# Two convolutional bottleneck layers on one core: stage borders with statistics summarized ahead, first images normalized on two engines, a plain first tile in the fused stage, and a divided last store

## Chip, cores and metric

The kernel runs on one core of a Trainium2 chip. The metric is device time in microseconds (us) of one execution. The engines are named as in the profile: PE (matmul), PEld (weight load, beside PE), DVE (vector), ACT (scalar), POOL (GpSimd), SP (sync); "ACTq" and "SPq" are the sequencers of ACT and SP while they issue transfers. The "granted clock" is the share of PE's full clock that the profile records; "half clock" is 0.50 of it.

## The reference

Two identical layers follow each other. Cut to what matters:

```python
# x: (64, 1024, 14, 14) fp32; P = 256
def layer(x, w1, b1, g1, be1, w2, b2, g2, be2, w3, b3, g3, be3, residual_scale):
    out = relu(bn(conv(x,   w1, b1, 1x1), g1, be1))    # 1024 -> 256
    out = relu(bn(conv(out, w2, b2, 3x3), g2, be2))    # 256 -> 256
    out = bn(conv(out, w3, b3, 1x1), g3, be3)          # 256 -> 1024
    return relu(x + softplus(residual_scale)[0] * out)
# bn: mean and variance over the whole batch and both image axes
```

A batch norm over the whole batch is a barrier: no value of the next convolution may be normalized before the last value of this one is known. These barriers are the "borders" of this document.

## The kernel before

Images are taken in pairs, as T = 32 tiles of PX = 392 pixels, and 256 channels lie in two slots of 128 partitions. Conv1 runs as sums of products with fewer multiplications (`Conv1`, seven products instead of eight), conv2 as a Winograd-like scheme over groups of 8 images (`combine`, `products`, `finish`). The statistics of conv3 are not taken from its output but from a Gram matrix of its input (`gram`, `conv3_stats`), so that in layer 0 conv3, the residual and conv1 of layer 1 run interleaved, in the "fused" stage. In layer 1 the last stage is conv3 and the residual alone. These are the parts that the change touches.

```python
# ---- border conv1 -> conv2, and conv2 -> gram: all 32 statistics, then ten tiny operations
def aggregate(stats, n):
    mv = small.tile(...)
    for o in range(n):
        nc.vector.bn_aggr(mv[:, o, :], stats[:, o, :, :].rearrange("p t f -> p (t f)"))
    return mv

def affine(mv, n, par, g, be, conv_bias=None):
    # ... tiles cut
    nc.vector.tensor_scalar(v, mv[:, :, 1], EPS, None, ALU.add)
    nc.scalar.activation(sd, v, AF.Sqrt)
    nc.vector.reciprocal(r, sd)
    # ... one Newton step, scale, shift: eight more operations on DVE, cut

# ---- start of conv2: both slots normalized on ACT, then combined
norm(0, aff)
ahead, acc = combine(*pairs[0]), None

# ---- end of each group in conv2 (finish, pair (0, 5)): statistics after the last row
nc.vector.tensor_add(out_rows[0], a, fa)
nc.vector.tensor_add(out_rows[3], d[:, :, :full], fb[:, :, :full])
for o in range(MS):
    y = y_grp[:, o, g].rearrange("p h l -> p (h l)")
    for c in range(GI // G):
        nc.vector.bn_stats(stats[:, o, g * (GI // G) + c, :], y[:, c * PX : (c + 1) * PX])

# ---- after conv2: loads for the next stages, then the scale and shift
w3 = load_w3(one, b)                  # issued by SP
if b == 0:
    w1 = load_w1(one, b + 1)          # four transfers, issued by ACT
aff = affine(aggregate(stats2, MS), MS, pb, G2, BE2)
# ...
crow = pool.tile([P, M], FP, tag="crow", name="crow")
nc.sync.dma_start(out=crow, in_=pars[b][:, NPAR:])     # subtracted in gram
# ...
made = [conv3(psum, 0, o, w3) for o in range(2)] if b == 1 else ()

# ---- fused stage: conv3 runs 28 + 14 steps alone before conv1 joins
a, c = stream(first_convs()), stream(last_convs())
step = 7 * CS // 2
for i in range(step + LAG):
    next(c)

# ---- a tile of the last stage ends with one store, issued by GpSimd
nc.gpsimd.dma_start(out=out[t], in_=xt.rearrange("p s f -> p (s f)"))
```

## Time and profile before

| | before |
|---|---|
| median of 4 runs (of the later comparison) | 2213.81 us |
| span of the profiled execution | 2210.7 us |
| first matmul | 6.67 us |
| conv1 of layer 0 ends on PE | 312.20 us |
| PE gap conv1 to conv2, layers 0 and 1 | 12.52 and 12.65 us |
| conv2 end to first transpose of gram, layers 0 and 1 | 11.00 and 10.91 us |
| last gram product to first conv1 matmul, layer 0 | 40.23 us |
| last relu to end of span | 9.89 us |

The table is read off the timeline of PE: a gap is the time from the end of one matmul to the start of the next. The prediction shows the timelines inside these gaps. The list of waits of PE: its columns are the waiting group, what ended the wait, the total in us, how often, and the longest:

```profile
PE ps L470 <- DVE sums L450: 25.2, 2, 12.7
PE ps L583 <- ACT y L396: 22.4, 4, 11.0
```

Line 470 is the first matmul of conv2 and line 583 a transpose of gram. Two waits of conv2, one for each layer, are 25.2 us, and the waits of the transposes 22.4 us. The list shows no slow clock and no thin stretch: the 40 us before the fused stage hardly appear here; what fills them has to be read from the table of stretches.

### The profile page before, as it was taken

The numbers are of one execution on the slowest core, as the hardware profiler recorded it, in microseconds if no ns is written. First come the engines' busy times: TensorE is split into PE (matmuls) and PEld (weight loads), VectorE is DVE, ScalarE is ACT, GpSimd is POOL, SyncE is SP. The second block draws the span as 40 slices with busy tenths as digits, with TensorE's granted clock in tenths as the row PEclk, the third lists the DMA queues.
The fourth block names the chain that finished last, engine by engine and source line by source line (L and its number), as shares of the span: only waits on it lengthen the run. The fifth ranks groups of instructions, "written<-read, shape, count | busy, mean of one in ns | idle before, by whom it ended". The sixth has DMA issues, their size and how long they took to land.

```text
span 2210.7 us, 27233 instructions
## 1 busy us (share of the span) xinstructions
PE 2125.5 (96%) x10648; PEld 1808.1 (82%) x10648; DVE 1431.1 (65%) x2591; ACT 724.5 (33%) x1391; POOL 250.9 (11%) x350
## 2 busy tenths in 40 slices
PE   8999979999998989999999999799999799999997
PEld 4555549999997879999999999699999797555554
DVE  5676557788775656676666666678878544444443
ACT  1111133111105045555555555611111221444443
POOL 0000000000001133333333333000000000000000
PEclk9999989999999989999999999899999899999999
DMA  7655424555534424444444442355555501778874
GB/s 288 254 200 201 173 94 178 186 198 183 187 141 161 153 100 167 172 175 172 165 164 172 176 175 117 148 191 191 191 190 191 197 13 57 294 302 310 314 295 175
DMA packets 44289, 409.44 MB, mean 185 GB/s; under 512 B 5504, under 2 KB 5760, under 8 KB 11392
## 3 DMA queue, kind: packets, MB, share of 16 engines
q1 hardware_dynamic: 29664, 287.06, 35.6%
q0 software_dynamic: 8448, 67.11, 7.4%
q10 hardware_dynamic: 6048, 53.52, 5.8%
q8 instruction: 84, 1.38, 0.3%
q14 instruction: 45, 0.37, 0.0%
HBM read 289.18 MB, written 118.49 MB: 184 GB/s over the span
## 4 chain that ended last, share of the span: by engine, by line
PE 72%; issue 20%; DVE 4%; DMA 2%; POOL 1%; ACT 1%; POOLq 0%; SPq 0%; ACTq 0%
PE ay L135 14%; PE cy L135 7%; PE ap L135 7%; PE ps L481 6%; PE ps L475 6%; PE ps L470 6%; PE ps L477 6%; PE ps L483 6%; PE cp L135 4%; PE ax L135 3%; PE cx L135 2%; PE bx L571 2%; PE ps L135 1%; DMA y<-in_w 1%; PE bp L572 1%
## 5 line engine op out<-in xcount | busy, mean ns | idle before, releaser
L135 PE MATMUL ps<-y,w 128*128 128x392 f32 x1024 | 339.1, 494 | 0.0
L135 PEld LDWEIGHTS ps<-y,w 128*128 128x128 f32 x1024 | 195.2, 191 | 142.8 <-issue 1.5
L645 DVE SCALAR_TENSOR_TENSOR x<-ps,scale,x 128x392 f32<-128x392 f32 x256 | 159.7, 625 | 174.2 <-PE ps L135 174.2
L234 ACT ACTIVATE cu<-cy,scale 128x196 f32<-128x196 f32 x384 | 158.7, 423 | 227.9 <-PE cy L135 225.4
L646 ACT ACTIVATE x<-x,shift 128x392 f32<-128x392 f32 x256 | 158.9, 622 | 177.4 <-DVE x L645 177.4
L135 PE MATMUL ay<-at,w1s 128*128 128x196 f32 (+1 forms) x752 | 209.7, 382 | 1.2 <-ACT au L234 1.0
L503 DVE TENSOR_TENSOR f<-ps,ms 128x448 f32<-128x448 f32 x192 | 113.3, 600 | 148.7 <-PE ps L483 80.7
L470 PE MATMUL ps<-sums,u 128*128 128x224 f32 (+1 forms) x768 | 172.1, 347 | 25.2 <-DVE sums L450 25.2
L475 PE MATMUL ps<-r,u 128*128 128x224 f32 (+1 forms) x768 | 173.6, 347 | 0.0
L481 PE MATMUL ps<-r,u 128*128 128x224 f32 (+1 forms) x768 | 173.3, 347 | 0.0
L494 ACT ACTIVATE ms<-ps 128x448 f32<-128x448 f32 (+1 forms) x80 | 42.0, 525 | 392.2 <-PE ps L470 392.2
L135 PEld LDWEIGHTS ay<-at,w1s 128*128 128x128 f32 x752 | 136.0, 190 | 36.6 <-ACT au L234 4.6
L470 PEld LDWEIGHTS ps<-sums,u 128*128 128x128 f32 x768 | 137.3, 190 | 26.3 <-ACT t L410 13.1
L234 ACT ACTIVATE x<-x,shift 128x392 f32<-128x392 f32 x256 | 145.5, 614 | 31.1 <-POOL x L367 29.3
L477 PE MATMUL ps<-r,u 128*128 128x192 f32 (+1 forms) x768 | 154.1, 322 | 0.0
L483 PE MATMUL ps<-r,u 128*128 128x192 f32 (+1 forms) x768 | 153.3, 321 | 0.0
L367 POOL TENSOR_TENSOR x<-x,cu 128x392 f32<-128x392 f32 x128 | 130.6, 1021 | 189.3 <-DVE x L341 187.0
L341 DVE SCALAR_TENSOR_TENSOR x<-cp,scale,x 128x196 f32<-128x196 f32 x256 | 106.8, 417 | 67.2 <-PE cp L135 67.2
L475 PEld LDWEIGHTS ps<-r,u 128*128 128x128 f32 x768 | 141.8, 190 | 1.3
L481 PEld LDWEIGHTS ps<-r,u 128*128 128x128 f32 x768 | 137.0, 189 | 1.5
L477 PEld LDWEIGHTS ps<-r,u 128*128 128x128 f32 x768 | 132.9, 189 | 1.1
L483 PEld LDWEIGHTS ps<-r,u 128*128 128x128 f32 x768 | 132.0, 188 | 1.1
(161 smaller groups left out, 3666.4 us busy)
## 6 DMA issues: line engine op xcount, KB each, us to landing
u<-u SPq DMA_DIRECT2D x96, 1280.0 KB, 5.5
x<-in_x SPq DMA_DIRECT2D x62, 1568.0 KB, 6.6
mid<-x ACTq DMA_DIRECT2D x32, 1568.0 KB, 5.1
x<-mid SPq DMA_DIRECT2D x32, 1568.0 KB, 6.6
out<-x POOLq DMA_DIRECT2D x32, 1568.0 KB, 6.2
u<-y POOLq DMA_DIRECT2D x24, 320.0 KB, 6.5
u<-spare POOLq DMA_DIRECT2D x24, 320.0 KB, 3.0
x<-in_x SPq DMA_DIRECT2D x4, 784.0 KB, 6.6
```

The costliest lines, as they stand in the source:

```text
L135: tc.keep_in_program_order(nc.tensor.matmul(*args, **kw))
L234: tc.keep_in_program_order(nc.scalar.activation(*args, **kw))
L341: nc.vector.scalar_tensor_tensor(v, bank, self.scale[:, o : o + 1], v, ALU.mult, ALU.add)
L367: nc.gpsimd.tensor_add(v, v, self.u12)
L470: nc.tensor.matmul(m[:, o, :n], w(s, D1D2), sums[:, s].rearrange("p l c -> p (l c)"), start=(s == 0), stop=(s == MS - 1),)
L475: nc.tensor.matmul(odd, w(s, D1), r[:, s, :, WH:], start=(s == 0), stop=False)
L477: nc.tensor.matmul(odd[:, :, : WH - 1], w(s, D3), r[:, s, :, WH + 1 :], start=False, stop=(s == MS - 1))
L481: nc.tensor.matmul(even, w(s, D2), r[:, s, :, :WH], start=(s == 0), stop=False)
L483: nc.tensor.matmul(even[:, :, 1:], w(s, D0), r[:, s, :, : WH - 1], start=False, stop=(s == MS - 1))
L503: nc.vector.tensor_tensor(f[:, o].rearrange("p r (i q c) -> p q (r i) c", i=GI, q=2)[:, :, :lines], eos[o][:, :, :n].rearrange("p q (l c) ...
L645: nc.vector.scalar_tensor_tensor(v, ps, scale[:, o : o + 1], v, ALU.mult, ALU.add)
L646: nc.scalar.activation(v, v, AF.Relu, bias=shift[:, o : o + 1])
```

## The change

The intent is to shorten the serial chain at each border. The kernel's author describes it so: borders between stages, with statistics summarized ahead, first images normalized on two engines, first fused tile plain; sums of conv1 not pinned. (The diff does not touch the sums of conv1, so that last point has nothing of its own to test.) Two more edits are in the diff: the very first tile is loaded in four parts, and the last store is divided in four and moved from GpSimd to SP. The core of the diff; the reworked PSUM pools and the reordering inside `combine` and `products` are cut.

```diff
-    def aggregate(stats, n):
+    def summarize(stats, half, end, count):       # early statistics -> one entry
+        ...
+    def aggregate(stats, first):
+        n = stats.shape[1]
         for o in range(n):
-            nc.vector.bn_aggr(mv[:, o, :], stats[:, o, :, :].rearrange("p t f -> p (t f)"))
+            nc.vector.bn_aggr(mv[:, o, :], stats[:, o, first:, :].rearrange("p t f -> p (t f)"))
@@ affine: sqrt reads mv directly, eps as bias; two multiplications joined
+        nc.scalar.activation(sd, mv[:, :, 1], AF.Sqrt, bias=eps)
         nc.vector.tensor_scalar(v, mv[:, :, 1], EPS, None, ALU.add)
-        nc.scalar.activation(sd, v, AF.Sqrt)
@@ start of conv2
-        norm(0, aff)
-        ahead, acc = combine(*pairs[0]), None
+        half = 8
+        norm(0, y_grp[:, 0, 0], aff)                              # ACT, slot 0
+        norm_vector(1, y_grp[:, 1, 0, :half], aff)                # DVE, half of slot 1
+        ahead = combine(*pairs[0], lambda: norm(1, y_grp[:, 1, 0, half:], aff))
+        acc = None
...
-            acc = finish(g, pair, products(now), acc)
+            acc = finish(g, pair, products(now, k == 0), acc)     # first: slot by slot
@@ end of a group in conv2: a statistic per row and slot, rows 1 and 2 already earlier
+                for item, f, more, k in zip(done, (fa, fb), acc, (0, 3)):
+                    n = RT if k == 0 else full
+                    for o in range(MS):
+                        column(item, f, o)
+                        nc.vector.tensor_add(out_rows[k][:, o], more[:, o, :n], f[:, o, :n])
+                        stat(o, k)
+                if g == NG - 2:
+                    summarize(stats, 4 * (NG // 2), 4 * (NG - 1), GPX // 4)
@@ gram: the first normalization in two pieces
+                if normed == 0:
+                    px.insert(1, CH * P)
@@ gram to fused: the first tile as in layer 1, without the seven-product scheme
-                    made = [conv3(psum, 0, o, w3) for o in range(2)] if b == 1 else ()
+                    made = [conv3(psum, 0, o, w3) for o in range(2)]
+                first = residual(psum, xpool, b, 0, w3, aff, made)
@@ fused
-            for t in range(T):
+            for t in range(1, T):
-        step = 7 * CS // 2
-        for i in range(step + LAG):
+        for i in range(LAG):
@@ residual, last tile
+        step = 2 if b == 1 and t == T - 1 else CS
...
+            if (o + 1) % step == 0:
+                queue = nc.gpsimd if step == CS else nc.sync
@@ start
-        pair = [load_x(xpool, 0, t, 2) for t in range(2)]
+        pair = [load_x(xpool, 0, t, 4 if t == 0 else 2) for t in range(2)]
```

## The prediction

> **What bounds the kernel now.** I read the engine table first, then the list of who waited for whom (PE alone), then a table of stretches cut at the gaps of PE, then the timeline inside each gap. The engine table says who leads:
>
> ```profile
> PE 2125.5 (96%) x10648; PEld 1808.1 (82%) x10648; DVE 1431.1 (65%) x2591; ACT 724.5 (33%) x1391; POOL 250.9 (11%) x350
> ```
>
> PE is busy for 2125.5 of 2210.7 us, so only 85 us of idle time can be won, plus what PE loses when it restarts slowly. Inside a stage nothing can be won: the table of stretches has PE at 69.00 of 69.00 us within conv2. The same table, cut at the borders (columns: stretch, its length, busy time of PE, PEld, DVE, ACT, POOL, granted clock, DMA share, GB/s):
>
> ```profile
> 312.20:324.70 12.50, 0.00 (x0) 0.01 (x1) 8.47 (x21) 10.24 (x11) 0.00 (x0) 0.68 0.80 315
> 324.70:331.00 6.30, 6.28 (x19) 5.85 (x20) 6.30 (x11) 6.30 (x8) 0.00 (x0) 0.54 0.00 1
> 660.40:671.40 11.00, 0.01 (x1) 0.03 (x1) 8.76 (x24) 2.04 (x3) 0.20 (x4) 0.71 0.73 273
> 780.10:806.50 26.40, 19.06 (x85) 15.48 (x86) 17.87 (x51) 12.88 (x30) 9.32 (x11) 0.85 0.32 123
> 1401.00:1413.65 12.65, 0.00 (x0) 0.03 (x1) 9.27 (x22) 8.95 (x10) 0.00 (x0) 0.68 0.78 311
> 1749.40:1760.20 10.80, 0.00 (x0) 0.00 (x0) 8.69 (x24) 1.94 (x3) 0.20 (x4) 0.71 0.78 308
> ```
>
> Four gaps of 11 to 12.7 us with no PE work, each followed by some 6 us at about half clock (0.54), and one thin stretch of 26 us. What fills a gap is the timeline (start, length, engine, line, operation). Conv1 to conv2, layer 0:
>
> ```profile
> 312.84 1.28 ACT L701 ACT_TABLE_LOAD   x1
> 313.45 1.02 DVE L689 BATCH_NORM_AGGREGATE mv<-stats 128x2 f32<-128x192 f32 x1
> 316.53 4.86 ACT L396 ACTIVATE y<-y,shift,scale 128x1568 f32<-128x1568 f32 x3 [1.61 <-DVE shift L717]
> 321.99 1.09 DVE L426 TENSOR_TENSOR r<-t 128x896 f32<-128x896 f32 x1
> 324.72 1.83 PE L470 MATMUL ps<-sums,u 128*128 128x224 f32 x4 [12.52 <-DVE sums L450]
> ```
>
> It is one serial chain: aggregate all 32 statistics, ten tiny operations 0.2 us apart, two normalizations of 1.69 us, combination, column sums, first matmul. Conv2 to gram, layer 0:
>
> ```profile
> 660.98 0.86 DVE L534 TENSOR_TENSOR y<-fb,f 128x672 f32<-128x672 f32 x1
> 661.88 3.84 DVE L538 BATCH_NORM_STATS2 stats<-y 128x6 f32<-128x392 f32 x8
> 665.63 1.89 DVE L689 BATCH_NORM_AGGREGATE mv<-stats 128x2 f32<-128x192 f32 x2
> 669.57 3.28 ACT L396 ACTIVATE y<-y,shift,scale 128x1568 f32<-128x1568 f32 x2 [1.61 <-DVE shift L717]
> 671.40 1.30 PE L583 MATMUL ps<-ident,y 128*128 128x128 f32 x5 [11.00 <-ACT y L396]
> ```
>
> Here 5.7 us are statistics.
>
> **The Trainium skill.** (1) "TensorE: Matmul & The Clock Gate", What's actually happening: after an idle window of about 3.4 us, free running, the clock is halved until a busy window. The trace agrees: 0.54 after the gap, 1.00 from 331 us. So shorter gaps of 5 to 7 us still pay the slow restart. (2) "VectorE: DVE Perf Modes", The perf-mode tier table: tensor_scalar on fp32 in SBUF runs at 2x, tensor_tensor at 1x. Trace: tensor_scalar 128x256 took 288 ns, tensor_tensor 128x448 617 ns. (3) "ScalarE: Activation LUTs", What ACT_TABLE_LOAD costs: 1283 ns; the trace has the same, at 312.84. (4) "DMA: Bandwidth & Descriptors", Anatomy of one DMA: about 2 us fixed per transfer, so a short last transfer cannot fall below that; the last store of before landed 5.4 us after its issue.
>
> **Part by part.**
>
> *Conv1 to conv2, layer 0.* Aggregating 3 entries (one a summary) in place of 32: 1.02 us to about 0.15 (estimate, in proportion to elements). But the square root must wait for the table load, to 314.12, so it starts at 314.13 and not 314.71; with it seven more steps of 0.2 us and not eight: shift ready at 315.75, not 316.53, 0.8 us won. Then: ACT normalizes slot 0 (1.69) while DVE does 896 elements of slot 1 in two tensor_scalars (0.62 each by the 288 ns row, estimate), hidden. DVE then combines slot 0 alone: two stt (0.50 + 0.43) and a half-size add (0.62). PE can start with the eight slot-0 products at 1.69 + 0.95 + 0.62 + 0.1 = 3.35 us after shift, where before it took 8.2. Slot 1 is ready some 1.6 us later, while these 16 instructions at half clock take 5.7 us, so PE is then fed. PE starts at 319.1, not 324.72: **5.6 us**.
>
> *The same border, layer 1.* No table load: the first aggregate (1400.77) no longer delays the last statistics, the second shrinks by 0.87, v is off the chain: shift at 1403.9 and not 1405.33. PE at 1407.2, not 1413.65: **6.4 us**.
>
> *Conv2 to gram.* The eight statistics after the last row become one per half row: behind the last product come a column (0.51), an add of 336 (0.45), one statistic (0.45), two aggregates of 5 entries (0.2 each). But the four statistics of rows 1 and 2 (1.9 us) now lie ahead, in a stretch where DVE has little room (654.1 end of the pair before): I get the last statistic at 661.9, shift at 664.0 and not 669.57: 5.5 us. The split of the first norm lets PE start 0.5 us after shift and not 1.8, but slot 1's rest still comes 3.75 us after; worth 0 to 1 us. Against it: the subtraction after the transposes needs crow, whose transfer is issued at 662.4 whatever DVE does:
>
> ```profile
> DMA to landing us min/median/max: 4.7/5.5/6.4
> ```
>
> (for crow, 6.4 in layer 0, 4.7 in layer 1). It lands near 668.5; first gram product at 669.5, not 674.67: **5.2 us**, and in layer 1 at about 1757.8, not 1763.57: **5.7 us**.
>
> *Gram to the fused stage.* Before, from the last gram product (766.2) to the first conv1 matmul (806.5) are 40.2 us: statistics 13.9, then 42 steps of conv3 alone, with 13.9 us of PE work (0.33 us a step) in 26.4: 2.9 us waiting for the scale, half clock, and waits of 0.9 to 2.2 us on the loop PE, ACT, DVE, POOL. After: layer 1 of before already shows what this becomes. There, two plain products stand ahead of the statistics, and gram end to the end of the tiny products took 1850.0 to 1863.15 = 13.1 us with them; the plain tile followed without a gap, 24 instructions of 0.33 us plus 1.9 for the slow clock = 9.8. Then only 14 steps of conv3 run alone; the steady rate alone was 3.13 us for 7 steps, with the conv1 sums in the way 7 to 8 us. Sum 13.1 + 9.8 + 7.5 = 30.4, against 40.2: **10 us**, 7 to 13. The plain tile costs 10.5 us of PE and not 9.2, which is in this sum. The lead of conv3 over conv1 stays 14 steps into tile 1, so the tail is as before.
>
> *Start.* The first tile in quarters: before, the first matmul waited for its weights (6.67 us) that shared the transfer engines with x rows of 6.3 KB; with rows of half that, perhaps 2 us earlier, at half clock, and part is lost again behind later tiles: **0.6 us**.
>
> *End.* The last tile leaves in four stores. The last is 392 KB and not 1568: 2.2 us of transfer and 0.2 of issue saved: **2.4 us**.
>
> *Hidden.* The summaries (four aggregates of some 0.5 us and small operations, 3 us of DVE per stage) run where DVE is 65 to 78% busy; statistics per row have the same elements. The sums of conv1 are not touched by the diff; unpinned, the scheduler may place them differently.
>
> Sum: 5.6 + 6.4 + 5.2 + 5.7 + 10 + 0.6 + 2.4 = 35.9 us. From 2214.1 that is 2178; I say **2179**, for small new stalls.
>
> **Rivals.** (a) A transfer replaces the chain. The conv2 filters land 5.8 us after issue at the earliest:
>
> ```profile
> DMA to landing us min/median/max: 5.8/8.0/10.6
> ```
>
> that is 318.1 and about 1406.9, only 1.0 and 0.3 us ahead of my PE starts. If these or crow land later, 3 to 6 us of the gain go: 2183. (b) DVE becomes the bound at the borders: the 2x mode fails for the half normalization, or DVE drags the extra statistics; 1 us per border: 2184. For it: DVE is 79% busy at the end of conv2. Against it: the largest costs removed are DVE's own. (c) The shorter gaps escape the half clock: five restarts at 2.5 us each would give up to 10 us more, about 2169. Against it: gaps of 4 to 7 us contain an idle window nearly always. (d) The fused lead-in stalls as before on its loop: loss of 5 us, 2184.
>
> **Range and chances.** The borders go by about 1 us each, together, and the fused lead-in by 3; with the clock's phase 3 more. So 2171 to 2189. Faster by over 2% needs under 2169.8, that is 44 us, over half of all idle time: 0.08. Slower needs a broken schedule: 0.01.
>
> **What would show it.** PE gaps: about 6.9 us at both conv1 borders and 4 to 5 at both conv2 borders; sqrt right after the table load in layer 0; the subtraction of gram waiting for crow; 28 to 32 us from last gram product to first conv1 matmul; conv2 still without PE waits; 2 us less after the last matmul; half clock still at each border. Wrong would be: conv2 or the fused stage longer by over 2 us, or restarts with no half clock.

## The result, and the profile after

| | before | after |
|---|---|---|
| median | 2213.81 us (2212.21 to 2214.30, 4 runs) | 2177.43 us (2175.48 to 2178.76, 4 runs) |
| ratio | | 0.9836, 95% interval 0.9819 to 0.9853 |
| span of the profiled execution | 2210.7 us | 2175.1 us |
| mean granted clock | 0.983 | 0.990 |

A ratio is the mean time of one kernel's runs over that of the other's of the same rounds, so it is not quite the ratio of the medians. The gain of 36.4 us, or 1.6%, lies within the 2% that count as the same.

The engine table of the changed kernel:

```profile
PE 2123.2 (98%) x10624; PEld 1802.2 (83%) x10624; DVE 1432.1 (66%) x2648; ACT 720.8 (33%) x1387; POOL 243.6 (11%) x342
```

PE's busy time fell by only 2.3 us (the prediction shows 2125.5), while the span fell by 35.6. So nearly all that was won is idle time of PE: 85.2 us before, 51.9 us after. The waits of PE in the changed kernel, with the columns as before:

```profile
PE ps L513 <- DVE r L454: 14.1, 2, 7.3
PE cp L622 <- DVE zt L642: 6.2, 5, 1.6
...
PE cy L640 <- ACT y L401: 6.0, 1, 6.0
PE ps L640 <- ACT y L401: 5.5, 3, 4.8
```

The first line stands where 25.2 us stood: conv2 now starts after the combined rows of slot 0 (line 454) and no longer after the column sums. The waits of the transposes (line 640) fell from 22.4 us to 12.0: 6.0 and 5.5 in the two rows shown, and 0.5 in a third. The gap in conv1 to conv2 of layer 0 and what follows it, as a table of stretches (stretch, length, busy time of PE, PEld, DVE, ACT, POOL, granted clock, DMA share, GB/s), with the stretch between gram and the fused stage below:

```profile
312.32:319.62 7.30, 0.00 (x0) 0.00 (x0) 5.41 (x17) 5.83 (x10) 0.00 (x0) 0.69 0.81 311
319.62:326.00 6.38, 6.38 (x20) 6.05 (x21) 6.28 (x10) 6.38 (x7) 0.00 (x0) 0.55 0.62 263
759.53:789.20 29.67, 27.99 (x122) 18.82 (x121) 18.54 (x52) 7.79 (x17) 2.63 (x3) 0.94 0.28 109
```

The same view of the kernel before, for the last of these stretches:

```profile
766.25:806.48 40.23, 32.34 (x146) 25.80 (x146) 23.04 (x65) 13.14 (x31) 9.30 (x11) 0.83 0.21 80
```

Between gram and the fused stage PE is busy for 4.35 us less and idles 6.2 us less (7.9 us before, 1.7 after): together the 10.6 us. Less busy time is not only less work: its clock there is also higher, 0.94 against 0.83. After the gap of conv1 to conv2, the clock is still about half (0.55) for 6 us.

Inside the first border (start, length, engine, line, operation; in square brackets, how long the engine had been idle and what ended that):

```profile
312.96 1.28 ACT L783 ACT_TABLE_LOAD   x1
...
313.58 0.24 DVE L772 BATCH_NORM_AGGREGATE mv<-stats 128x2 f32<-128x18 f32 x1
...
314.26 0.29 ACT L783 ACTIVATE sd<-mv,eps 128x2 f32<-128x2 f32 x1
...
315.96 0.75 DVE L405 TENSOR_SCALAR y<-y,scale,shift 128x896 f32<-128x896 f32 x1
...
318.95 0.62 DVE L454 TENSOR_TENSOR r<-t 128x448 f32<-128x448 f32 x1
319.62 1.75 PE L513 MATMUL ps<-r,u 128*128 128x224 f32 x4 [7.30 <-DVE r L454]
```

The aggregate reads 18 numbers and not 192 (three entries of six), and takes 0.24 us where 1.02 stood. The square root now starts 0.02 us after the table load has ended, so the load, and not the aggregate, sets the chain. DVE's half of slot 1 takes 0.75 us (and 0.63 for its second operation), hidden beside ACT. The one addition ahead of PE covers 448 elements, not 896.

The second border, conv2 to gram in layer 0, same columns:

```profile
656.76 2.08 ACTq L118 DMA_DIRECT2D w<-in_w  x4
...
657.18 0.29 DVE L772 BATCH_NORM_AGGREGATE mv<-stats 128x2 f32<-128x30 f32 x1
...
658.88 0.29 ACT L783 ACTIVATE sd<-mv,eps 128x2 f32<-128x2 f32 x1 [5.22 <-issue]
...
663.91 0.29 DVE L890 TENSOR_SCALAR crow<-crow 128x256 f32<-128x256 f32 x1 [3.36 <-DMA crow<-in_par]
...
665.15 1.20 PE L622 MATMUL cp<-zt 128*128 128x257 f32 x2 [1.57 <-DVE zt L642]
```

Two things stand here that the kernel before did not show as a loss. The aggregate is done at 657.47, but the square root runs only at 658.88, right after ACT's sequencer has issued four weight transfers (656.76 to 658.84). And DVE waits 3.36 us for the transfer of `crow`.

A third thing is in no wait: the clock after the restart. The table of stretches for the first 10 us from the first transpose on, in layer 0 and layer 1, columns as above, for the kernel before:

```profile
671.40:681.40 10.00, 9.78 (x55) 8.50 (x56) 6.40 (x13) 10.00 (x10) 1.08 (x2) 0.81 0.19 76
1760.10:1770.10 10.00, 9.61 (x42) 8.14 (x43) 2.72 (x4) 10.00 (x8) 0.00 (x0) 0.63 1.00 425
```

And for the changed kernel:

```profile
661.33:671.33 10.00, 7.95 (x31) 6.48 (x32) 3.73 (x7) 7.33 (x8) 0.54 (x1) 0.56 0.68 264
1729.89:1739.89 10.00, 9.26 (x47) 7.64 (x48) 3.40 (x6) 10.00 (x8) 0.00 (x0) 0.74 1.01 420
```

The granted clock (the third number from the end) fell from 0.81 to 0.56 in layer 0 and rose from 0.63 to 0.74 in layer 1. In layer 0 the half clock lasts 10.24 us in both kernels, read off stretches of 0.1 us. Before, 6.4 us of it passed in the gap, where a slow clock costs nothing, and 3.8 fell on work; now 1.5 pass in the gap and 8.8 fall on work.

The account of the whole span, from the two traces, in us:

| part | before | after | won | predicted |
|---|---|---|---|---|
| start to end of conv1, layer 0 | 312.20 | 312.32 | −0.1 | 0.6 |
| gap conv1 to conv2, layer 0 | 12.52 | 7.30 | 5.2 | 5.6 |
| conv2, layer 0 | 335.68 | 335.67 | 0.0 | 0 |
| conv2 end to gram end, layer 0 | 105.85 | 104.24 | 1.6 | 5.2 |
| gram end to first conv1 matmul | 40.23 | 29.67 | 10.6 | 10 |
| fused stage to end of conv1, layer 1 | 594.5 | 594.8 | −0.3 | 0 |
| gap conv1 to conv2, layer 1 | 12.65 | 6.81 | 5.8 | 6.4 |
| conv2, layer 1 | 335.65 | 334.29 | 1.4 | 0 |
| conv2 end to gram end, layer 1 | 100.90 | 94.08 | 6.8 | 5.7 |
| conv3 statistics and residuals, layer 1 | 349.3 | 350.9 | −1.6 | 0 |
| PE end to end of span | 11.2 | 5.0 | 6.2 | 2.4 |
| sum | | | 35.6 | 35.9 |

The sum agrees to 0.3 us, but two terms are off by 3.6 to 3.8 us in opposite directions: conv2 to gram in layer 0, and the end. Two smaller ones, 1.4 and −1.6, are the clock: in conv2 of layer 1 the half clock covers 5.7 us of work before and 2.9 after, and in the last stage it lasts 3.41 us before and 6.83 after; each microsecond of it costs about half a microsecond. The experiments go for these two first, and for whether each part of the change earns its term.

### The profile page after: what moved, and what is told of

Its sections match the earlier page's. It is cut to its first block, busy times and chain, and to the rows that moved or that the text cites. A ratio compares the mean times of both kernels' runs of the same rounds, so it can differ in the third digit from the quotient of the medians.

```text
span 2175.1 us, 27250 instructions
## 1 busy us (share of the span) xinstructions
PE 2123.2 (98%) x10624; PEld 1802.2 (83%) x10624; DVE 1432.1 (66%) x2648; ACT 720.8 (33%) x1387; POOL 243.6 (11%) x342
## 3 DMA queue, kind: packets, MB, share of 16 engines
q8 instruction: 84, 1.38, 0.3%
## 4 chain that ended last, share of the span: by engine, by line
PE 93%; DVE 3%; DMA 1%; ACT 1%; issue 0%; POOL 0%; SPq 0%; DVEq 0%; ACTq 0%
PE ps L513 23%; PE ps L144 17%; PE ay L144 15%; PE cy L144 8%; PE ap L144 8%; PE ps L494 6%; PE ax L144 4%; PE cp L144 4%; PE cp L622 4%; PE cx L144 2%; PE ap L623 2%; PE ps L640 1%; DMA y<-in_w 1%; DVE spare L170 0%; ACT y L401 0%
## 5 line engine op out<-in xcount | busy, mean ns | idle before, releaser
L513 PE MATMUL ps<-r,u 128*128 128x224 f32 (+3 forms) x3072 | 561.3, 334 | 14.1 <-DVE r L454 14.1
L513 PEld LDWEIGHTS ps<-r,u 128*128 128x128 f32 x3072 | 535.1, 189 | 19.8 <-DVE r L454 7.9
L239 ACT ACTIVATE cu<-cy,scale 128x196 f32<-128x196 f32 x372 | 154.0, 423 | 221.2 <-PE cy L144 221.2
L373 POOL TENSOR_TENSOR x<-x,cu 128x392 f32<-128x392 f32 x124 | 125.9, 1015 | 187.6 <-DVE x L347 187.6
L622 PE MATMUL cp<-zt 128*128 128x257 f32 x392 | 119.9, 387 | 6.5 <-DVE zt L642 6.2
L144 PE MATMUL cy<-ct,w3s 128*128 128x196 f32 x496 | 123.0, 330 | 1.4 <-ACT cu L239 1.4
L239 ACT ACTIVATE au<-ay 128x196 f32<-128x196 f32 (+1 forms) x141 | 53.8, 381 | 178.4 <-PE ay L144 175.8
L144 PE MATMUL ap<-x,w1s 128*128 128x196 f32 (+1 forms) x376 | 107.7, 390 | 4.9 <-DVE y L285 4.9
L401 ACT ACTIVATE y<-y,shift,scale 128x1568 f32<-128x1568 f32 (+2 forms) x68 | 103.1, 1585 | 5.6 <-DVE shift L801 5.6
L144 PE MATMUL ay<-x,w 128*128 128x196 f32 (+1 forms) x376 | 104.8, 381 | 0.0
```

The costliest lines, as they stand in the source:

```text
L144: tc.keep_in_program_order(nc.tensor.matmul(*args, **kw))
L239: tc.keep_in_program_order(nc.scalar.activation(*args, **kw))
L373: nc.gpsimd.tensor_add(v, v, self.u12)
L401: nc.scalar.activation(y, y, AF.Relu, bias=shift[:, s : s + 1], scale=scale[:, s : s + 1])
L513: nc.tensor.matmul(to, u[:, s, o, k], v, start=start, stop=stop, skip_group_check=by_slot)
L622: nc.tensor.matmul(g0, zt[:, c, 0:P], zt[:, c, :], start=first, stop=last)
```

## The experiments

Twelve runs were made, eleven of varied kernels and one of the changed kernel again, all with correct results. The medians of the kernel before in the three series were 2214.15, 2213.05 and 2212.80 us. The interval of each ratio is about ±0.0015, or 3 us, so differences of 1 to 3 us are read from the traces and not from the times. No experiment differs from the kernel before by over 2%.

### Each part undone: `u_plain`, `u_norm`, `u_stats`

`u_plain` sends the first tile of the fused stage through the seven-product scheme again.

```diff
-        xs = [first, load_x(xpool, 0, 1)]
+        xs = [load_x(xpool, 0, 0)]
-            for t in range(1, T):
+            for t in range(T):
-        for i in range(LAG):
+        for i in range(7 * CS // 2 + LAG):
-                    made = [conv3(psum, 0, o, w3) for o in range(2)]
+                    made = [conv3(psum, 0, o, w3) for o in range(2)] if b == 1 else ()
-                first = residual(psum, xpool, b, 0, w3, aff, made)
+                first = residual(psum, xpool, b, 0, w3, aff, made) if b == 1 else None
```

> The changed kernel with the fused stage begun as before (no plain first tile, no two products ahead of the small statistics products, conv3 42 steps ahead again). Theory of the prediction: the plain tile is worth about 10 us (in the trace of the changed kernel 29.8 us from the last gram product to the first conv1 matmul, before 40.2), so this run is at about 2187 us and shows 39 to 41 us there. Rival: only a new luck of the clock and not the order of work made the difference; then this run is within 3 us of 2177.

Measured: 2184.76 us, ratio 0.9871 (0.9856 to 0.9885), 7.3 us over the changed kernel. The stretch from the last gram product to the first conv1 matmul, columns as before:

```profile
759.95:798.36 38.41, 30.69 (x145) 24.25 (x145) 22.80 (x64) 13.22 (x31) 9.27 (x11) 0.87 0.22 84
```

It is 38.41 us against 29.67, so 8.7 us of the 10.6 go with the plain tile and its two products in this pair of traces. PE's idle time is back at 7.7 us: in this stretch PE waits 5.0 us for ACT's `cu` and 2.2 for DVE's `x`, as before the change (4.9 and 2.2), where the changed kernel has 1.4 and 0.3. The same stretch in the twelve traces with the plain tile takes 29.66 to 32.95 us (30.9 on average), by the clock alone, as `crow_early` will show; so the tile is worth 5.5 to 8.7 us by the traces, and 7.3 by the times. The remaining 1.8 us against the kernel before are mostly the clock: its half lasts 10.24 us here and 13.65 there, by an estimate 1.7 us. The expected 39 to 41 us and 2187 us were a little too high.

`u_norm` lets ACT normalize the whole of slot 1 again, combines both slots at once and starts conv2 in the old order of products.

```diff
-        norm_vector(1, y_grp[:, 1, 0, :half], aff)
-        ahead = combine(*pairs[0], lambda: norm(1, y_grp[:, 1, 0, half:], aff))
+        norm(1, y_grp[:, 1, 0], aff)
+        ahead = combine(*pairs[0])
...
-            acc = finish(g, pair, products(now, k == 0), acc)
+            acc = finish(g, pair, products(now, False), acc)
```

> The changed kernel with the first group of conv2 normalized whole on one engine and combined whole, products in the plain order. Theory: from shift ready to the first conv2 matmul 8.1 us again and not 3.7, so 4.5 us at each of the two borders, 9 us in all, about 2186 us. Rival: the slow restart hides part (PE at half clock for 3.4 to 6.8 us whatever happens), or the filters' transfer (landing 5.4 to 5.8 us after its issue) sets the start already; then the loss is under 5 us.

Measured: 2186.56 us, ratio 0.9875 (0.9860 to 0.9890), 9.1 us over the changed kernel. The start of conv2 in layer 0 in its timeline:

```profile
323.98 1.83 PE L494 MATMUL ps<-sums,u 128*128 128x224 f32 x4 [11.82 <-DVE sums L437]
```

The gaps are 11.82 and 11.33 us against 7.30 and 6.81, so the split is worth 4.5 us at each of the two borders, and 2 × 4.5 is the whole loss. The old gaps were 12.52 and 12.65; the shorter aggregate and `affine` are therefore worth the other 0.7 us in layer 0, where the table load covers the aggregate, and 1.3 us in layer 1.

`u_stats` takes the statistics of conv2 after the last row again, eight of them per group, and aggregates all 32.

```diff
-                for item, f, more, k in zip(done, (fa, fb), acc, (0, 3)):
-                    ...                                  # column, add, stat per row
+                a, d = acc
+                nc.vector.tensor_add(out_rows[0], a, fa)
+                nc.vector.tensor_add(out_rows[3], d[:, :, :full], fb[:, :, :full])
+                for o in range(MS):
+                    ...                                  # bn_stats per 392 pixels
...
-            aff = affine(aggregate(stats2, 4 * (NG - 1) - 1), MS, pb, G2, BE2)
+            aff = affine(aggregate(stats2, 0), MS, pb, G2, BE2)
```

> The changed kernel with the statistics of conv2 taken and aggregated as before (eight after the last row, 32 entries aggregated), everything else kept. Theory of the prediction: shift of the conv2 to gram borders is 5.5 us later each, worth 5.2 and 5.7 us, about 2188 us. What the trace of the changed kernel suggests: in layer 0 the square root already waits 1.35 us behind the issue of weights on ACT's queue and the subtraction waits for crow, so undoing costs only about 2 us in layer 0 and 6.5 in layer 1, about 2186 us.

Measured: 2184.97 us, ratio 0.9867 (0.9851 to 0.9884), 7.5 us over the changed kernel. From the end of conv2 to the first transpose it takes 9.60 and 9.51 us (layers 0 and 1) and not 6.04 and 4.79; to the end of gram 106.63 and 99.75 and not 104.24 and 94.08. So the statistics are worth 5.7 us in layer 1, and only 2.4 us in layer 0. One reason its timeline of the border in layer 0 shows:

```profile
654.97 2.10 ACTq L118 DMA_DIRECT2D w<-in_w  x4
...
658.61 1.88 DVE L766 BATCH_NORM_AGGREGATE mv<-stats 128x2 f32<-128x192 f32 x2
...
660.53 0.30 ACT L777 ACTIVATE sd<-mv,eps 128x2 f32<-128x2 f32 x1 [8.77 <-DMA w<-in_w]
```

With the long statistics, ACT's issue of four transfers ends at 657.07, long before the aggregate does at 660.49; it is hidden. With the short ones it is not (the changed kernel's timeline above: aggregate done at 657.47, issue done at 658.84). The removed work had covered another cost, which now stands on the chain.

### The shortfall at conv2 to gram, layer 0: `w1_sync`, `crow_early`, `crow_w1`

The prediction named one thing that would cap the gain here: the subtraction needs `crow`, which lands late. The rival is ACT's issue of the weight transfers of layer 1, which only layer 0 has. `w1_sync` moves that issue to SP, after `crow`.

```diff
-    def load_w1(pool, b):
+    def load_w1(pool, b, queue=nc.scalar):
-                nc.scalar.dma_start(out=w[:, o, h], in_=w1s[b][:, o, h])
+                queue.dma_start(out=w[:, o, h], in_=w1s[b][:, o, h])
...
-            if b == 0:
-                w1 = load_w1(one, b + 1)
             aff = affine(aggregate(stats2, 4 * (NG - 1) - 1), MS, pb, G2, BE2)
...
                     nc.sync.dma_start(out=crow, in_=pars[b][:, NPAR:])
+                    if b == 0:
+                        w1 = load_w1(one, b + 1, nc.sync)
```

> The changed kernel with layer 1's conv1 weights issued on the sync queue behind crow and not on ACT's queue. Theory: in layer 0 the square root no longer waits behind the four issues (2.08 us on ACT), shift comes 1.35 us earlier; but crow's landing still sets the first gram product, so the first product moves by under 0.5 us and the total by under 1 us. Rival: ACT's issue is the whole cause of the missing 3.4 us in layer 0; then the first gram product comes 1.3 us earlier and the total falls by 1 to 3 us.

Measured: 2176.10 us, ratio 0.9831 (0.9816 to 0.9846). Its timeline at that border:

```profile
657.65 0.29 DVE L772 BATCH_NORM_AGGREGATE mv<-stats 128x2 f32<-128x30 f32 x1
657.98 0.30 ACT L783 ACTIVATE sd<-mv,eps 128x2 f32<-128x2 f32 x1 [3.84 <-DVE mv L772]
```

The square root now follows the aggregate at once and waits for nothing else. The first transpose comes 4.67 us after the end of conv2 and not 6.04, and gram ends 101.42 us after it and not 104.24. The first gram product comes 8.73 us after the end of conv2 and not 9.87: the theory that `crow` sets it failed, and the rival is nearer. Of the 2.8 us, 1.4 are the wait itself, and about 1.0 come from the clock, by an estimate from its mean over the first 10 us after the restart (0.66 against 0.56): the half clock lasts 6.83 us in this execution, and 10.24 in that of the changed kernel.

Yet the whole kernel gained only 1.3 us, which is within the noise of the times. The next stretch, with the same instructions to within the records that a trace may lose, is now longer:

```profile
757.17:788.50 31.33, 29.66 (x120) 19.83 (x120) 18.62 (x52) 7.88 (x17) 2.63 (x3) 0.89 0.27 103
```

31.33 us against 29.67, at a clock of 0.89 against 0.94. Part of the gain was given back to the clock.

`crow_early` gives `crow` a place for the whole kernel and loads it before conv2. To make room, two small tiles got one buffer and not two (96 and 32 bytes per partition).

```diff
+        crow = keep.tile([P, M], FP, tag="crow", name="crow")
+        nc.sync.dma_start(out=crow, in_=pars[b][:, NPAR:])
         with tc.tile_pool(name=f"conv2_{b}", bufs=1) as pool, ExitStack() as scope:
...
-                    crow = pool.tile([P, M], FP, tag="crow", name="crow")
-                    nc.sync.dma_start(out=crow, in_=pars[b][:, NPAR:])
```

> The changed kernel with crow loaded before conv2 (in a tile that lives throughout). Theory: the subtraction no longer waits for crow (3.4 us of DVE waiting in layer 0, 3.0 in layer 1), gram's first product comes 1 to 2 us earlier in each layer, 2 to 3 us in all, about 2174.5. Rival: the second half of the first normalization (3.8 us after shift) sets the pace anyway; then under 1 us.

Measured: 2176.11 us, ratio 0.9834 (0.9819 to 0.9849). The wait of DVE for `crow` is gone in both layers (3.36 and 2.99 us before), and the first gram product comes 1.6 to 1.9 us earlier relative to the end of conv2. But gram ends 103.12 and 94.12 us after conv2 against 104.24 and 94.08: 1.1 us better in layer 0, of which about 0.3 are the clock, and nothing in layer 1. In layer 0 PE had stood 1.57 us before its first product (665.15 above); in layer 1 it had transposes to do meanwhile. `crow` is a small part of the shortfall, and the expected 2 to 3 us did not come. The stretch to the fused stage was 32.95 us in this execution:

```profile
757.29:790.24 32.95, 31.27 (x122) 21.77 (x120) 18.62 (x52) 7.88 (x17) 2.62 (x3) 0.84 0.57 232
```

The three values 29.67, 31.33 and 32.95 go with clocks of 0.94, 0.89 and 0.84. The half-clock stretches at the borders and in this stage have lengths that are multiples of 3.41 us (3.41, 6.83, 10.24 and 13.65 occur); each costs about half of itself, and the steps of 1.6 to 1.7 us between the three values are one such window each. The twelve traces with the plain tile have these values five, five and two times; `again`, the changed kernel unaltered, has 29.66.

`crow_w1` has both edits, with the weights issued from SP at the old place of `crow`.

```diff
+        crow = keep.tile([P, M], FP, tag="crow", name="crow")         # before conv2
+        nc.sync.dma_start(out=crow, in_=pars[b][:, NPAR:])
...
-            if b == 0:
-                w1 = load_w1(one, b + 1)
...
-                    nc.sync.dma_start(out=crow, in_=pars[b][:, NPAR:])
+                    if b == 0:
+                        w1 = load_w1(one, b + 1, nc.sync)
```

> The changed kernel with both: the weights off ACT's queue and crow loaded before conv2. From the end of conv2 to the last gram product layer 0 took 106.0 us before, 104.2 changed, 103.1 with crow early, 101.4 with the weights moved. If the two waits are in series, both together give about 100; if crow hides behind the weights' issue and the pace of the first normalizations, 101 to 102, as with the weights alone.

Measured: 2175.43 us, ratio 0.9832 (0.9817 to 0.9847). Conv2 end to gram end is 100.99 us in layer 0 and 94.06 in layer 1: within 0.5 us of `w1_sync` alone in layer 0. So the two waits are not in series: once the issue is moved, `crow` costs little.

What the traces agree on is a sum of two terms: the shortening of the gap ahead of the first transpose, and the clock in the first 10 us after it. The second term is an estimate: 10 us times the difference of the mean clock from that of the kernel before (0.81 in layer 0, 0.63 in layer 1). In us:

| kernel, layer | gap saved | clock in 10 us | clock term | sum | measured to gram end |
|---|---|---|---|---|---|
| changed, 0 | 5.0 | 0.56 | −2.5 | 2.5 | 1.6 |
| `w1_sync`, 0 | 6.3 | 0.66 | −1.5 | 4.8 | 4.4 |
| `crow_early`, 0 | 4.9 | 0.59 | −2.2 | 2.7 | 2.7 |
| `u_stats`, 0 | 1.4 | 0.60 | −2.1 | −0.7 | −0.8 |
| changed, 1 | 6.1 | 0.74 | +1.1 | 7.2 | 6.8 |

The sums come within 0.9 us of what was measured, and the changed kernel, with `crow` late, falls 0.9 short in layer 0. So, of the 6.3 us by which the gap shrinks once the issue is moved, layer 0 loses 1.4 to the issue on ACT's sequencer, 2.5 to more work at half clock, and about 0.9 to `crow`; 1.6 are left. The clock's part could not be switched off by itself; the table is one reading that fits five cases.

Two things limit it. The work at half clock after the restart of gram was 3.8 us in layer 0 of the kernel before, but 7.3 in its layer 1, and 8.1 and 7.4 in `u_stats`, whose gaps are long too (9.60 and 9.51 us). So a long gap does not by itself keep the half clock off the work; the 3.8 is the odd value, and there is no second trace of the kernel before to tell whether it recurs. And not all of the clock is chance: in layer 0 the half clock lasts 10.24 us in all nine traces with the short statistics and the issue on ACT, and 6.83 in all three with the issue moved, so the 1.0 us of clock in the gain of `w1_sync` came each time.

### The end: `one_pool`, `four_pool`, `one_sync`

The change differs from before in two ways at the end: four stores and not one, and SP and not GpSimd. The three kernels complete the square.

```diff
 # one_pool: one store, GpSimd
-        step = 2 if b == 1 and t == T - 1 else CS
+        step = CS
 # four_pool: four stores, GpSimd
-                queue = nc.gpsimd if step == CS else nc.sync
+                queue = nc.gpsimd
 # one_sync: one store, SP
-        step = 2 if b == 1 and t == T - 1 else CS
+        step, last = CS, b == 1 and t == T - 1
-                queue = nc.gpsimd if step == CS else nc.sync
+                queue = nc.sync if last else nc.gpsimd
```

> The changed kernel with the last tile stored at once through the gpsimd queue as before. Prediction: 2.4 us lost (transfer size alone). Trace: 9.9 us from the last relu to the end before, 3.7 after, so 6.2 us lost, about 2183.5 us.

> The changed kernel with the last tile in four stores, all through the gpsimd queue and not the sync queue. If the size of the last store is what counts (the prediction), the end is within 0.5 us of the changed kernel's 3.7 us after the last relu. If the queue counts (a fixed end of the gpsimd queue of some 3.5 us), it is about 7 us.

> The changed kernel with the last tile stored at once through the sync queue. If size alone counts: 9.9 us after the last relu as before. If the queue counts: about [...]7 us or less.

| | one store | four stores |
|---|---|---|
| GpSimd: last relu to end of span | 9.82 us (`one_pool`; before: 9.89) | 8.55 us (`four_pool`) |
| SP: last relu to end of span | 6.85 us (`one_sync`) | 3.73 us (changed kernel) |
| GpSimd: median time | 2183.37 us, ratio 0.9861 (0.9847 to 0.9876) | 2181.53 us, 0.9855 (0.9839 to 0.9871) |
| SP: median time | 2180.11 us, ratio 0.9851 (0.9836 to 0.9865) | 2177.43 us, 0.9836 |

By the trace, the queue is worth 3.0 us for one store and 4.8 for four, and the size 1.3 us on GpSimd and 3.1 on SP. The issues of the last stores in the DMA view of the end (out, queue, number, KB each, median us from issue to landing), for the kernel before:

```profile
out<-x POOLq DMA_DIRECT2D x1, 1568.0 KB, 5.4
```

And for `one_sync`:

```profile
out<-x SPq DMA_DIRECT2D x1, 1568.0 KB, 5.1
```

The landing differs by only 0.3 us between the queues; the last of four stores landed 2.6 us after its issue in both `four_pool` and the changed kernel. So it isn't the transfer. The last store of before was issued at 2201.09 and landed, by this row, about 2206.5; the span ended at 2210.7, some 4 us later. In `one_sync` the store was issued at 2171.35, landed about 2176.4, and the span ended at 2178.2, under 2 us later. The Trainium skill, "DMA: Bandwidth & Descriptors", Latency and other measured facts, gives the first byte of a transfer about 0.6 us when SP or ACT issues it and about 1 us from GpSimd. The landings agree with a difference of that order; the 3.0 to 4.8 us at the end are something else.

What the program still waits for after a GpSimd store stands in the kept traces, in the view of the line that closes the program (859 before, 950 after). GpSimd has instructions named DRAIN there; the columns are the shortest, middle and longest of three in ns, and the first and last start. For `before`, `four_pool`, the changed kernel and `one_sync`, in this order:

```profile
L859 POOLq DRAIN x3: 40/102/8730, 2201.1 to 2210.3; - x3
L950 POOLq DRAIN x3: 40/102/7496, 2172.2 to 2180.2; - x3
L950 POOLq DRAIN x3: 40/102/10507, 2161.1 to 2174.9; - x3
L950 POOLq DRAIN x3: 40/93/9537, 2161.1 to 2177.9; - x3
```

The long one can only be the first, and it begins with GpSimd's last store. In `before` it ends at 2209.8, 3.3 us after the landing, and the span 0.9 us after that; in `four_pool` it ends at 2179.7 and the span at 2180.5; `one_pool` has the same picture (8.79 us, ending 0.8 us before the span). With the last store on SP, GpSimd's last store is that of the tile before, and the DRAIN has ended (2171.7 and 2170.6) before the last store lands. So the DRAIN of GpSimd closes the program in the three kernels with its store at the end, and the queue matters because of it. Why it outlasts the landing, the traces do not show.

### The start: `x_two`, and the changed kernel once more: `again`

`x_two` loads the first tile in two parts, as before the change; `again` is the changed kernel unaltered, in the same rounds.

```diff
-        pair = [load_x(xpool, 0, t, 4 if t == 0 else 2) for t in range(2)]
+        pair = [load_x(xpool, 0, t, 2) for t in range(2)]
```

> The changed kernel with the first tile loaded in halves as before. Prediction: 0.6 us lost. Trace of the changed kernel: the first matmul is 0.6 us earlier but conv1 of layer 0 ends 0.1 us later than before, so the quarters are worth nothing: first matmul near 6.5 us, end of conv1 within 0.5 us of the changed kernel's 312.3, total the same within the scatter.

> The changed kernel once more, unaltered, as the yardstick of this call. About 2177 us. It also tests the clock: from the last gram product of layer 0 to the first conv1 matmul the runs so far had 29.7, 31.3 or 32.9 us with the same instructions. If that is the phase of the half clock alone, this run falls on one of these steps and the sum over all stages moves by up to 3 us between executions.

Measured: `again` 2177.10 us, ratio 0.9840 (0.9825 to 0.9854); `x_two` 2180.16 us, ratio 0.9853 (0.9837 to 0.9870). In the traces the first matmul starts at 6.76 us (6.06 in the changed kernel), and conv1 of layer 0 ends at 313.68, against 312.32 and, in `again`, 311.53. So quarters are worth 1.4 to 2.2 us beside these two, and 3 in the times; but the kernel before, with halves too, ended conv1 at 312.20. The twelve traces with quarters end conv1 between 310.93 and 312.74 us, 311.8 on average. One execution of a start scatters by as much as the effect, and the size of this term is not settled beyond "0 to 3 us"; the expectation that quarters are worth nothing did not hold in the times, where the runs of `x_two` and `again` do not overlap. `again` also shows what a trace alone can't: its conv2 in layer 1 took 335.85 us, as before the change, so the 1.4 us "won" there in the account above are luck of the clock.

### A version on top: `sqrt_w1`

In layer 0 the first square root waits for its table, at 312.96 in the changed kernel. `sqrt_w1` is `w1_sync` with both layers' softplus ahead of the loop and a dummy square root behind them, so that the table is loaded early.

```diff
+    sps = [softplus(p) for p in par]
+    warm = small.tile([P, 1], FP, tag="warm", name="warm", bufs=1)
+    nc.vector.tensor_add(warm, sps[0], sps[1])
+    nc.scalar.activation(warm, warm, AF.Sqrt)
     for b in range(2):
-        pb = par[b]
-        sp = softplus(pb)
+        pb, sp = par[b], sps[b]
...                                       # and the edits of w1_sync
```

> The weights off ACT's queue, and a square root done once during conv1 so that its table is loaded ahead of the first border. Theory: the conv1 to conv2 gap of layer 0 shrinks from 7.3 to the 6.8 us of layer 1, where no table is loaded. Total about 2175.5, the fastest of all; rival: the table is loaded again at the border, or the filters' transfer then ends the wait, and the gap stays at 7.3.

Measured: 2174.75 us (2173.71 to 2176.02), ratio 0.9829 (0.9814 to 0.9844): the lowest median of all, 2.4 us under `again` of the same rounds, though the intervals overlap. Its timeline:

```profile
14.86 1.28 ACT L868 ACT_TABLE_LOAD   x1
...
312.49 0.29 ACT L783 ACTIVATE sd<-mv,eps 128x2 f32<-128x2 f32 x1 [0.91 <-DVE mv L772]
...
317.86 1.43 PE L513 MATMUL ps<-r,u 128*128 128x224 f32 x3 [6.90 <-DVE r L454]
```

The table is loaded at 14.86 us, and the square root waits for the aggregate alone. The gap is 6.90 us and not 7.30: 0.4 us for a load of 1.28, because most of it lay beside the last statistics anyway.

## Why the prediction was right, and where it was not

The total was right: 2179.0 was said, 2177.43 came, inside the range, with the class "within 2%". By its own steps:

- **What bounds the kernel** held. The gain is idle time of PE (33 of the 36 us), and no stage got longer by more than 0.3 us except the last, by one window of half clock (1.6 us).
- **Conv1 to conv2**: 5.6 and 6.4 were said, 5.2 and 5.8 came. In layer 0 PE restarted at 319.62 where 319.1 was said; the square root did follow the table load, and DVE's half was hidden. `u_norm` gives 4.5 us of each to the split.
- **Conv2 to gram**: in layer 1, 5.7 said and 6.8 came; in layer 0, 5.2 said and 1.6 came. **The step that failed** is "first gram product at 669.5, not 674.67: **5.2 us**": it took the time of the first product for the gain. That product did come 9.86 us after conv2's end, where 14.27 stood and 9.1 was said, but 2.8 of these 4.4 us were lost again by the end of gram. The prediction wrote that shorter gaps "still pay the slow restart", and so counted the restart as equal on both sides; it took "some 6 us at about half clock" after each gap from the one stretch that it had cut, while in its own kernel the four gaps are followed by 5.7, 3.8, 5.7 and 7.3 us. In layer 0 the 3.8 us of work at half clock became 8.8 (2.5 us by the estimate). In layer 1 the same term had the other sign. Its cap, "the subtraction after the transposes needs crow", was real in layer 0 but worth at most 1.1 us (`crow_early`). And the issue of four transfers on ACT's sequencer, 2.08 us, was missed: it delayed the square root by 1.4 us (`w1_sync`).
- **Gram to fused**: 10 said, 10.6 came; `u_plain` gives 5.5 to 8.7 of it to the plain tile, by the clock's step.
- **Start**: 0.6 said, −0.1 in one pair of traces, 1.4 to 2.2 in another; not settled.
- **End**: 2.4 said, 6.2 came. **The step that failed** is "2.2 us of transfer and 0.2 of issue saved": it counted the size of the last store and overlooked that its queue changes, and that the program ended with GpSimd's DRAIN and not with the landing. The landing did come 2.8 us sooner (5.4 and 2.6 us after the issue), but on GpSimd size alone is worth 1.3 us at the end, and the queue 4.8 more with four stores.
- **Hidden** work stayed hidden: conv2 took 335.67 us in layer 0, as before (335.68).
- The **rivals**: no transfer of conv2's filters took the chain's place (the waits of line 513 end on DVE); DVE's half normalization was fast enough; the half clock did stay, at all four borders of all 14 traces, though at some for fewer windows (6.83 us and not 13.65 at conv1 to conv2 of layer 1); it began 2.2 to 5.4 us after PE's last matmul, so that a gap need not contain a whole idle window of 3.41 us, as the prediction's reason has it; the fused lead-in did not stall. A wait did take the place of one removed, as rival (a) said in general, but the larger was an issue on an engine's own sequencer; the landing of `crow` came second.

So the sum was right partly by luck: two errors, 3.6 us too much and 3.8 too little, cancel, and so do 1.4 and −1.6 us of the clock in stages for which nothing was said; the other terms were within about 1 us each.

The parts undone one by one cost 7.3 (`u_plain`), 9.1 (`u_norm`), 7.5 (`u_stats`), 5.9 (`one_pool`) and 3.1 us (`x_two`, against `again`): 33.0 of 36.4. The rest fits the shorter aggregates and `affine` (0.7 and 1.3 us by the gaps of `u_norm`), within the clock's scatter.

## What to carry to other kernels

When a border between stages is shortened, list everything that the removed work used to cover, above all transfers that the engines of the chain issue themselves: their sequencers are on the chain too, and another queue may have room. Price a gain at the end of the stage that follows and not at its first instruction: after the restarts of these traces 2.9 to 8.8 us of work ran at half clock, and one trace of each kernel does not tell what will recur. At the end of a program, look at what ends last: here the DRAIN of GpSimd, so that the queue of the last store mattered more than its size.

## What the Trainium skill lacked or had wrong

- "DMA: Bandwidth & Descriptors" (Latency and other measured facts): it gives 0.4 us between the first bytes of the two kinds of queue. At the end of a program the runs show 3.0 us (one store of 1568 KB) and 4.8 us (four of 392 KB) between GpSimd and SP, with landings at most 0.3 us apart; no page tells of a long DRAIN of GpSimd from its last store on, 7.5 to 8.8 us where that store is the program's last.
- "DMA: Bandwidth & Descriptors" (Rules for kernel authors): that spreading transfers over queues "only saves sequencer issue time" is right, but the rule gives no time (elsewhere the page has only a count of sequencer cycles for earlier chips): here four transfers held ACT's sequencer for 2.08 us, and the square root behind them was 1.4 us late.
- "ScalarE: Activation LUTs" (What ACT_TABLE_LOAD costs): the load took 1.28 us as it says, but the further 1.38 us of drain did not appear: the load began 0.01 us after ACT's previous instruction and the next began 0.02 us after the load.
- "TensorE: Matmul & The Clock Gate" (What's actually happening): the window of 3.41 us is confirmed. The page has the clock halved after an idle window of that length; here it was halved 2.2 to 5.4 us after PE's last matmul. It puts the slow start at about 3.4 us; after the restarts here 2.9 to 8.8 us of work ran at half clock, 5.7 at conv1 to conv2 of layer 0 with PE busy throughout. That the same kernel varies with the phase of the window it says; what that costs a stage it does not: one stretch of nearly the same instructions took 29.66, 31.33 or 32.95 us.
